# Two heads in one product: attention of an eight-head Fourier layer with the heads on two halves of the rows

## The chip, the core and the metric

The kernel runs on one core of a Trainium2 chip. The metric is the time of one execution in microseconds of the device; lower is better. A core has five engines that run side by side: TensorE (PE in the profile) multiplies matrices into the PSUM memory, VectorE (DVE) and ScalarE (ACT) work element by element and read PSUM, GpSimd (POOL) works element by element on SBUF, and SyncE (SP) issues the transfers. A product on TensorE has two operands: the stationary one, loaded into the array as weights, and the moving one, which streams past it. The contraction runs over the rows (partitions) of both, at most 128. A product that needs only some rows and columns of the array can be given a place in it, so that products at different places run side by side.

## What is computed

Two layers of the same kind, one behind the other, on an input `x` of 2 batches, 56 channels and 128 x 128 points. Cut to what matters:

```python
B, K, H, W = x.shape            # 2, 56, 128, 128
A = Kw.shape[2]                 # 8 heads
xn = inorm(x.reshape(B * K, 1, H, W), g1, b1)
k, q, v = (fno_layer(xn, w, b, sw, sb) for ... in (K, Q, V))     # each 8 heads
scores = jnp.einsum('baks,bals->bakl', qh, kh) * scale           # over the 128 x 128 points
attn = jax.nn.softmax(scores, axis=-1)                           # 56 x 56 for each head
out = jnp.einsum('bakl,bals->baks', attn, vh)
out = fno_layer(out.reshape(B * K, A, H, W), Pw, Pb, Psw, Psb)   # 8 heads to one
att = inorm(out + x, gan, ban)
an = inorm(att, g2, b2)
h = fno_layer(an, M0w, ..., norm=True, act=True)
h = fno_layer(h, M1w, ..., norm=True, act=False)
y = inorm(h, gmo, bmo) + att
```

`fno_layer` is a spectral convolution on 32 x 16 complex Fourier modes plus a 1 x 1 convolution. Everything is fp32.

## The kernel before

The work is done on the modes, not on the points, wherever it can be. For a batch `b`, the tile `xf` holds the modes of the 56 channels: 128 rows (64 for each half `e` of the modes) by 8 groups of 56 channels. Each layer runs through these stages, for batch 0 and batch 1, one stage of one batch woven with another stage of the other batch (`_woven` takes pieces of both generators in turn, by the costs that they yield; a planner then orders the instructions of each engine and inserts the waits):

- `turn`, `modes_chain`: mean and variance, the forward transform into `xf`.
- `gram`, `gram_chain`: a 56 x 56 product of the channels over all points (L511: 128 products of 128 rows by 64 columns, alternately on the lower and upper half of the columns).
- `scores`: for each of 8 mode groups and 8 heads a product of weights with the modes (L595), copied by ACT (L600), and then the scores (L576). They gather in one PSUM bank, heads 0 to 3 on rows 0 to 55 and heads 4 to 7 on rows 64 to 119. At its start POOL writes two masks that hold a scaled identity for each head: SG (L569) and MI (L570), each 56 rows by 8 x 56.
- `values`: for each pair `t` of mode groups (4 of them), halves `e` and members `c` a product with all 8 heads at once (L617), 64 rows by 64 columns with 512 moving columns; ACT copies 128 x 1024 to VT (L622). The modes' group is what distinguishes the two halves of VT's rows. At its end 8 transposes (L626) and a copy (L627).
- `softmax_chain`: DVE and ACT turn the scores into weights; 16 products with the identity (L648) transpose them, each head on both halves of the rows of PSUM, and ACT copies 128 x 448 to AT (L653).
- `mix_chain`: 8 products of the mask MI with AT (L661), one for each head, contracting 56 rows, and one product of two identities (L662), all summed into one bank; then BT (DVE, L665), L668, BTx (ACT, L670), L672, gb (DVE, L674) and 8 products (L678) into a bank that stays in use until `norms_chain`.
- `heads`: for each `t`, head `a`, half `e` and member `c` a product of VT and AT (L689), 56 rows by 64 columns with 56 moving columns, at one of four quadrants of the array; 128 products for each batch, summed over the heads. ACT copies the sum to D (L697).
- `norms_chain`, `gelu`, `h_chain`, `end`: the norms, the two further convolutions, and the result. `inverse` (L401, L406) and `gelu`'s synthesis (L751, L766) need pairs of PSUM banks too.

An fp32 product of the code is two instructions on PE, with two loads of weights. PSUM is given out from two pools: `bank()`, 2 tiles of one bank, and `pair()`, 3 tiles of two banks. Before the change, the transposed weights (`softmax_chain`) and the sums of `heads` each take a pair; the scores, the products of `mix_chain` and those of the norms take single banks.

The order around the change, in each layer (L946 to L961): `gram_chain` of batch 1 with `scores` of batch 0; `softmax_chain` with `values` of batch 0; `mix_chain` with `heads` of batch 0; `norms_chain` of batch 0 with `scores`, then `softmax_chain` with `values`, then `mix_chain` with `heads` of batch 1; `norms_chain` of batch 1 with `gelu` of batch 0. In `mix_chain` with `heads`, a quarter of the heads' products stands after L662's bank is read, a quarter after L672, and the rest behind L678.

Of the kernel before, what the change touches and what calls it, by code (L numbers as in the profile page):

```python
# [39 lines left out]
ALU = mybir.AluOpType  # L40
# [126 lines left out]
def fno_layers(ctx: ExitStack, tc: tile.TileContext, x, out, weights, small, const):  # L167
# [441 lines left out]
    def values(L, b, st):  # L609
        R, xf = room(b), st["xf"]  # L610
        xv = grid(xf[:, :448])
        for t in range(4):
            p = pair()
            for e in range(2):
                for c in range(2):
                    o = K * (2 * t + c)
                    T.matmul(  # L617
                        p[64 * c : 64 * c + 64, e, :], lhsT=xf[64 * e : 64 * e + 64, o : o + 64],
                        rhs=WTv[64 * e : 64 * e + 64, 2 * t + c].rearrange("p a m -> p (a m)"), start=True, stop=True,
                        tile_position=(64 * e, 64 * c), skip_group_check=True,  # L620
                    )
            S.copy(R["VT"][:, t], p.rearrange("p e m -> p (e m)"))  # L622
            yield 1.0
        p = pair()
        for t in range(8):
            T.transpose(p[:K, t // 4, N * (t % 4) : N * (t % 4) + N], xv[:, t, :], ident)  # L626
        S.copy(R["XT"][:K].rearrange("p t m -> p (t m)"), p[:K].rearrange("p j m -> p (j m)"))  # L627
        yield 0.8

    def softmax_chain(L, b, st):  # L630
        R, sc = room(b), st["sc"]
        SC = R["SC"][:, :, :K]
        rl, rk = st["rr"][:, :K], st["rr"][:, K : K + 1]
        V.tensor_tensor(SC, grid(sc[:, :224], 4), _bc(rl, 1, 4), ALU.mult)
        top, tot = little(f"top{b}", [N, 4]), little(f"tot{b}", [N, 4])
        V.tensor_reduce(top, SC, AX.X, ALU.max)
        V.tensor_tensor(SC, SC, _bc(top, 2, K), ALU.subtract)
        S.activation(SC, SC, AF.Exp, scale=rk)
# [14 lines left out]
        S.activation(R["AT"].rearrange("p (c m) -> p c m", c=2), p[:, :, :224], AF.Copy, scale=rk)  # L653
        yield 1.0

    def mix_chain(L, b, st):
        R, gc = room(b), st["gc"]
        AT, MI, XT = grid(R["AT"]), R["MI"], R["XT"]
        p = bank()
        for a in range(HEADS):  # L660
            T.matmul(p[:K, :K], lhsT=MI[:K, a, :], rhs=AT[:K, a, :], start=(a == 0), stop=False)  # L661
# [18 lines left out]

    def heads(L, b, st):
        R = room(b)
        AT, VT = grid(R["AT"]), R["VT"].rearrange("p t (e m) -> p t e m", e=2)
        p = pair()
        for t in range(4):
            for a in range(HEADS):
                for e in range(2):
                    for c in range(2):
                        T.matmul(  # L689
                            p[64 * e : 64 * e + 64, c, K * t : K * t + K],  # L690
                            lhsT=VT[64 * c : 64 * c + K, t, e, 64 * a : 64 * a + 64],
                            rhs=AT[64 * c : 64 * c + K, a, :], start=(a == 0), stop=(a == 7),
                            tile_position=(64 * c, 64 * e), skip_group_check=True,
                        )
# [330 lines left out]
```

## Time and profile before

| what | value |
|---|---|
| median of 3 runs (lowest to highest) | 573.26 us (572.86 to 574.89) |
| the profiled execution | 573.63 us |
| its span, first to last instruction | 571.6 us |
| mean granted clock of TensorE | 0.882 |

The profile lists, for each engine, the time in which it was busy, and for groups of instructions the line of the code, the operation, the tiles with their shapes (`56*64 56x56` is 56 rows by 64 columns of weights and 56 rows by 56 moving columns), the count, the busy time and the mean length of one. A chain of waits follows the execution back from its end: each piece is what the next had to wait for. The granted clock is the share of full speed that TensorE is allowed; it changes during the execution. Instructions of PE overlap in its pipeline, so that the mean length of one says less than how many start in a given time.

### The profile page before, as it was taken

The page shows a single profiled execution, that of the slowest core. Times are in us where ns is not written, and L with a number is a line of the kernel's source. Part 1 is how long each engine was busy: PE and PEld are TensorE (multiplying, and loading weights), DVE is VectorE, ACT ScalarE, POOL GpSimd, SP SyncE. Part 2 cuts the span into 40 slices and gives each one's busy share as a digit, 9 for nine tenths or more (in the row PEclk, how much of TensorE's full clock was granted, in tenths as well). Part 3 has the DMA queues.
Part 4 walks back from the last instruction along what each step waited for, and adds up shares of the span by engine and source line. Part 5 has one row for each costly group of instructions (what it writes and reads, how often), then busy time and mean ns, then how long its engine had stood idle before and what let it go on. Part 6 is the DMA issues. An engine that isn't in the chain of part 4 may idle for free.

```text
span 571.6 us, 15727 instructions
## 1 busy us (share of the span) xinstructions
PE 468.0 (82%) x7110; PEld 323.5 (57%) x7110; DVE 334.5 (59%) x577; ACT 191.1 (33%) x238; POOL 181.9 (32%) x190
## 2 busy tenths in 40 slices
PE   2547988989989999799596769987998999979390
PEld 1423957659676556466562367756957655645250
DVE  0576488811626765858459985830251866686751
ACT  2334140152428556123104214124352755612000
POOL 2440517800090000064456841810000000016466
PEclk9999699887999998977577959987799999899587
DMA  8993000050000000056145441030000000006587
GB/s 203 211 195 43 4 2 4 4 140 4 1 4 2 1 2 1 1 168 189 47 128 152 139 131 7 4 102 2 3 1 3 2 1 1 2 18 203 186 252 278
DMA packets 16307, 40.64 MB, mean 71 GB/s; under 512 B 2528, under 2 KB 3296, under 8 KB 16224
## 3 DMA queue, kind: packets, MB, share of 16 engines
q1 hardware_dynamic: 15520, 38.25, 24.9%
q10 hardware_dynamic: 720, 1.39, 1.0%
q8 instruction: 56, 0.92, 0.7%
q14 instruction: 11, 0.09, 0.1%
HBM read 24.69 MB, written 14.68 MB: 69 GB/s over the span
## 4 chain that ended last, share of the span: by engine, by line
PE 48%; DVE 25%; DMA 8%; ACT 7%; issue 5%; POOL 4%; SPq 1%; POOLq 1%; ACTq 0%; DVEq 0%
PE pair L766 6%; PE pair L751 5%; PE pair L595 4%; PE pair L801 4%; PE pair L689 4%; DVE X L550 4%; DVE stats L373 4%; PE bank L576 3%; PE bank L511 3%; PE bank L789 2%; DVE P L916 2%; DMA X<-store 2%; PE bank L483 2%; PE bank L386 2%; DMA sm<-small 2%
## 5 line engine op out<-in xcount | busy, mean ns | idle before, releaser
L821 DVE BATCH_NORM_STATS2 stats<-P 128x6 f32<-128x512 f32 x64 | 40.4, 677 | 20.2 <-ACT P L819 20.1
L916 DVE SCALAR_TENSOR_TENSOR P<-P,hs,pair 128x1024 f32<-128x1024 f32 x32 | 40.0, 1271 | 19.9 <-PE pair L766 19.8
L918 POOL TENSOR_TENSOR X<-P,xr 128x1024 f32<-128x1024 f32 x16 | 39.4, 2466 | 31.1 <-DVE P L916 20.0
L550 DVE TENSOR_TENSOR X<-X,gvr 120x1024 f32<-120x1024 f32 x32 | 48.9, 1558 | 0.0
L373 DVE BATCH_NORM_STATS2 stats<-P 128x6 f32<-128x448 f32 x64 | 35.7, 611 | 21.5 <-ACT P L371 11.9
L819 ACT ACTIVATE P<-pair 128x1024 f32<-128x1024 f32 x32 | 32.7, 1027 | 32.1 <-PE pair L766 31.5
L395 POOL MEMSET WT<- 128x256 f32 x4 | 1.3, 313 | 124.7 <-PE bank L789 90.3
L801 PEld LDWEIGHTS pair<-C,P 120*128 120x128 f32 x256 | 27.5, 146 | 21.4 <-issue 11.5
L511 PE MATMUL bank<-P 128*64 128x56 f32 (+1 forms) x1024 | 38.7, 243 | 0.0
L511 PEld LDWEIGHTS bank<-P 128*64 128x64 f32 (+1 forms) x1024 | 37.1, 158 | 2.2 <-issue 1.9
L766 PE MATMUL pair<-X,Be 57*64 57x512 f32 x256 | 38.2, 692 | 0.0
L751 PE MATMUL pair<-C,WT 32*128 32x128 f32 x512 | 29.2, 333 | 10.7 <-DVE P L916 5.2
L766 PE MATMUL pair<-X,Bs 57*64 57x512 f32 x256 | 37.6, 628 | 0.0
L595 PEld LDWEIGHTS pair<-xf,WU 64*64 64x64 f32 x1024 | 33.3, 138 | 5.0 <-issue 4.1
L595 PE MATMUL pair<-xf,WU 64*64 64x56 f32 x1024 | 36.1, 223 | 0.0
L801 PE MATMUL pair<-C,P 120*128 120x120 f32 x256 | 35.4, 282 | 0.7 <-ACT P L819 0.5
L751 PEld LDWEIGHTS pair<-C,WT 32*128 32x128 f32 x512 | 23.6, 225 | 21.6 <-DVE P L916 7.2
L363 PE MATMUL pair<-C,X 56*128 56x56 f32 x256 | 17.8, 297 | 18.6 <-DMA X<-x 12.8
L802 ACT COPY WT<-pair 128x896 f32<-128x896 f32 x32 | 28.8, 907 | 12.2 <-PE pair L801 11.9
L341 POOL TENSOR_TENSOR WT<-tc,C 128x1024 f32<-128x1024 f32 x8 | 26.5, 3344 | 20.0 <-ACT tc L335 11.9
L371 ACT COPY P<-pair 128x896 f32<-128x896 f32 x16 | 14.4, 903 | 46.5 <-PE pair L365 45.7
L365 PE MATMUL pair<-C,X 120*128 120x120 f32 x128 | 20.5, 314 | 10.8 <-POOL X L918 9.0
(249 smaller groups left out, 881.2 us busy)
## 6 DMA issues: line engine op xcount, KB each, us to landing
X<-x SPq DMA_DIRECT2D x16, 448.0 KB
xr<-x SPq DMA_DIRECT2D x32, 224.0 KB
store<-X SPq DMA_DIRECT2D x32, 224.0 KB
out<-P SPq DMA_DIRECT2D x32, 224.0 KB
xr<-store SPq DMA_DIRECT2D x16, 224.0 KB
X<-store SPq DMA_DIRECT2D x16, 224.0 KB
C<-const_all ACTq DMA_DIRECT2D x1, 621.0 KB
stage<-weights ACTq DMA_DIRECT2D x1, 544.0 KB
```

The costliest lines, as they stand in the source:

```text
L373: V.bn_stats(stats[:, 2 * g + s, :], dst[:, 448 * s : 448 * s + 448])
L511: T.matmul(p[u : u + m, :K], lhsT=P[b][:, K * i : K * i + m], rhs=plane[b][:, i, :], start=(i < 2), stop=(i == N - 1), tile_position=(0, u ...
L550: V.tensor_tensor(v, v, _bc(st["gvr"][:120], 1, 8), ALU.mult)
L595: T.matmul(p[64 * e : 64 * e + 64, k, K * a : K * a + K], lhsT=WUv[64 * e : 64 * e + 64, t + k, a, :], rhs=xv[64 * e : 64 * e + 64, t + k, ...
L751: T.matmul(both[j // 2][:, j % 2, N * e : N * e + N], lhsT=Z[32 * j : 32 * j + 32, o : o + N], rhs=C["gw"][32 * j : 32 * j + 32, :], start ...
L766: T.matmul(p[64 * c : 64 * c + 64, r, :], lhsT=Bs[q, :], rhs=X2[q, b, s : s + 4, :].rearrange("p e w -> p (e w)"), start=False, stop=True, ...
L801: T.transpose(p[:, r, N * e : N * e + 120], h3[:120, o : o + N], ident[:120, :120])
L802: S.copy(hT[v].rearrange("p r e c k -> p (r e) c k"), p.rearrange("p r (e c k) -> p (r e) c k", e=4, c=2)[:, :, :, :K],)
L819: S.activation(h3, both[v].rearrange("p r m -> p (r m)"), AF.Gelu)
L821: V.bn_stats(stats[:, 4 * A + 2 * v + r, :], h3[:, 512 * r : 512 * r + 512])
L916: V.scalar_tensor_tensor(h3, h3, st["hs"], both[v].rearrange("p r m -> p (r m)"), ALU.mult, ALU.add)
L918: G.tensor_tensor(dst, h3, back(n), ALU.add)
```

## The change

The upper half of the rows no longer holds another group of modes but other heads: rows 0 to 63 hold heads 0 to 3, rows 64 to 127 heads 4 to 7, as in the scores. A product of `mix_chain` or `heads` then contracts two heads at once, over 128 rows.

- `values`: L617's 512 columns (8 heads) become two products of 256 columns (4 heads for each half of the rows), 32 products instead of 16 for each batch; VT keeps its size.
- `softmax_chain`: 8 transposing products instead of 16, each head only on its own half; one bank instead of a pair; the copy to AT is 128 x 224.
- `mix_chain`: 4 products with MI over 128 rows instead of 8 over 56. The product of identities runs over 128 rows.
- `heads`: 64 products of 128 rows by 64 columns, alternately on the two column halves of the array, instead of 128 products of 56 rows on four quadrants; one bank instead of a pair; the copy to D keeps its size and has plain order.
- `scores`: the mask MI is written by two POOL instructions of 64 rows by 4 x 56 instead of one of 56 rows by 8 x 56.

```diff
-            "AT": R[:, 5120:5568], "SC": grid(R[:, 6912:7168], 4), "SG": grid(R[:, 7168:7616]),
-            "MI": grid(R[:, 7616:8064]), "UX": [R[:, 896 * j : 896 * j + 896] for j in range(2)],
+            "AT": R[:, 5120:5344], "SC": grid(R[:, 6912:7168], 4), "SG": grid(R[:, 7168:7616]),
+            "MI": grid(R[:, 7616:7840], 4), "UX": [R[:, 896 * j : 896 * j + 896] for j in range(2)],
...
     def scores(L, b, st):
...
-        G.tensor_tensor(MI[:K], _bc(ident[:K, :K], 1, HEADS), _bc(d["mix"][:K], 2, K), ALU.mult)
+        for c in range(2):
+            q = slice(64 * c, 64 * c + 64)
+            G.tensor_tensor(MI[q], _bc(C["fold"][q, :K], 1, 4), _bc(d["mix"][q, 4 * c : 4 * c + 4], 2, K), ALU.mult)
...
     def values(L, b, st):
...
-            for e in range(2):
-                for c in range(2):
-                    o = K * (2 * t + c)
-                    T.matmul(
-                        p[64 * c : 64 * c + 64, e, :], lhsT=xf[64 * e : 64 * e + 64, o : o + 64],
-                        rhs=WTv[64 * e : 64 * e + 64, 2 * t + c].rearrange("p a m -> p (a m)"), start=True, stop=True,
-                        tile_position=(64 * e, 64 * c), skip_group_check=True,
-                    )
+            for u in range(2):
+                for e in range(2):
+                    for c in range(2):
+                        o = K * (2 * t + u)
+                        T.matmul(
+                            p[64 * c : 64 * c + 64, e, 256 * u : 256 * u + 256], lhsT=xf[64 * e : 64 * e + 64, o : o + 64],
+                            rhs=WTv[64 * e : 64 * e + 64, 2 * t + u, 4 * c : 4 * c + 4].rearrange("p a m -> p (a m)"),
+                            start=True, stop=True, tile_position=(64 * e, 64 * c), skip_group_check=True,
+                        )
...
     def softmax_chain(L, b, st):
...
-        p = pair()
+        p = bank()
         for a in range(4):
             for c in range(2):
-                for r in range(2):
-                    T.matmul(
-                        p[64 * r : 64 * r + 64, c, K * a : K * a + K], lhsT=R["SC"][64 * c : 64 * c + K, a, :],
-                        rhs=ident[64 * c : 64 * c + K, 64 * c : 64 * c + K], start=True, stop=True,
-                        tile_position=(64 * c, 64 * r), skip_group_check=True,
-                    )
-        S.activation(R["AT"].rearrange("p (c m) -> p c m", c=2), p[:, :, :224], AF.Copy, scale=rk)
-        yield 1.0
+                q = slice(64 * c, 64 * c + K)
+                T.matmul(
+                    p[64 * c : 64 * c + 64, K * a : K * a + K], lhsT=R["SC"][q, a, :], rhs=ident[q, q], start=True, stop=True,
+                    tile_position=(64 * c, 64 * c), skip_group_check=True,
+                )
+        S.activation(R["AT"], p[:, :224], AF.Copy, scale=rk)
+        yield 0.8
 
     def mix_chain(L, b, st):
...
-        for a in range(HEADS):
-            T.matmul(p[:K, :K], lhsT=MI[:K, a, :], rhs=AT[:K, a, :], start=(a == 0), stop=False)
-        T.matmul(p[:K, :K], lhsT=ident[:K, :K], rhs=ident[:K, :K], start=False, stop=True)
+        for a in range(4):
+            T.matmul(p[:K, :K], lhsT=MI[:, a, :], rhs=AT[:, a, :], start=(a == 0), stop=False)
+        T.matmul(p[:K, :K], lhsT=ident[:, :K], rhs=ident[:, :K], start=False, stop=True)
...
     def heads(L, b, st):
...
-        p = pair()
-        for t in range(4):
-            for a in range(HEADS):
+        p = bank()
+        for t in range(8):
+            for a in range(4):
                 for e in range(2):
-                    for c in range(2):
-                        T.matmul(
-                            p[64 * e : 64 * e + 64, c, K * t : K * t + K],
-                            lhsT=VT[64 * c : 64 * c + K, t, e, 64 * a : 64 * a + 64],
-                            rhs=AT[64 * c : 64 * c + K, a, :], start=(a == 0), stop=(a == 7),
-                            tile_position=(64 * c, 64 * e), skip_group_check=True,
-                        )
-            yield 1.4
+                    T.matmul(
+                        p[64 * e : 64 * e + 64, K * t : K * t + K], lhsT=VT[:, t // 2, e, t % 2, a, :], rhs=AT[:, a, :],
+                        start=(a == 0), stop=(a == 3), tile_position=(0, 64 * e), skip_group_check=True,
+                    )
+            if t % 2:
+                yield 1.0
...
-        S.copy(D.rearrange("p (t c k) -> p c t k", c=2, k=K), p[:, :, :224].rearrange("p c (t k) -> p c t k", t=4))
+        S.copy(D, p[:, :448])
```

More of the change, by code (lines that the diff above doesn't have):

```diff
@@ L642, in softmax_chain @@
         yield 4.5
-        p = pair()
+        p = bank()
         for a in range(4):
             for c in range(2):
-                for r in range(2):
-                    T.matmul(
-                        p[64 * r : 64 * r + 64, c, K * a : K * a + K], lhsT=R["SC"][64 * c : 64 * c + K, a, :],
-                        rhs=ident[64 * c : 64 * c + K, 64 * c : 64 * c + K], start=True, stop=True,
-                        tile_position=(64 * c, 64 * r), skip_group_check=True,
-                    )
-        S.activation(R["AT"].rearrange("p (c m) -> p c m", c=2), p[:, :, :224], AF.Copy, scale=rk)
-        yield 1.0
+                q = slice(64 * c, 64 * c + K)
[5 more added lines that the diff above has]
+        yield 0.8
     def mix_chain(L, b, st):
         R, gc = room(b), st["gc"]
-        AT, MI, XT = grid(R["AT"]), R["MI"], R["XT"]
+        AT, MI, XT = grid(R["AT"], 4), R["MI"], R["XT"]
         p = bank()
-        for a in range(HEADS):
-            T.matmul(p[:K, :K], lhsT=MI[:K, a, :], rhs=AT[:K, a, :], start=(a == 0), stop=False)
-        T.matmul(p[:K, :K], lhsT=ident[:K, :K], rhs=ident[:K, :K], start=False, stop=True)
+        for a in range(4):
+            T.matmul(p[:K, :K], lhsT=MI[:, a, :], rhs=AT[:, a, :], start=(a == 0), stop=False)
+        T.matmul(p[:K, :K], lhsT=ident[:, :K], rhs=ident[:, :K], start=False, stop=True)
         BT = little(f"BT{b}", [K, 64])
@@ L682, in heads @@
         R = room(b)
-        AT, VT = grid(R["AT"]), R["VT"].rearrange("p t (e m) -> p t e m", e=2)
-        p = pair()
-        for t in range(4):
-            for a in range(HEADS):
+        AT, VT = grid(R["AT"], 4), R["VT"].rearrange("p t (e u a m) -> p t e u a m", e=2, u=2, a=4)
+        p = bank()
+        for t in range(8):
+            for a in range(4):
                 for e in range(2):
-                    for c in range(2):
-                        T.matmul(
-                            p[64 * e : 64 * e + 64, c, K * t : K * t + K],
-                            lhsT=VT[64 * c : 64 * c + K, t, e, 64 * a : 64 * a + 64],
-                            rhs=AT[64 * c : 64 * c + K, a, :], start=(a == 0), stop=(a == 7),
-                            tile_position=(64 * c, 64 * e), skip_group_check=True,
-                        )
-            yield 1.4
+                    T.matmul(
[4 more added lines that the diff above has]
+                yield 1.0
         D = st["D"] = sp.tile([N, 448], F32, name=f"D{b}")
-        S.copy(D.rearrange("p (t c k) -> p c t k", c=2, k=K), p[:, :, :224].rearrange("p c (t k) -> p c t k", t=4))
+        S.copy(D, p[:, :448])
     def norms_chain(L, b, st):
```

## The prediction

> **What bounds the kernel now.** I read the page first, then the groups by line, then the chain of waits in the two stretches where the changed functions run, then windows with the granted clock.
>
> ```profile
> span 571.6 us, 15727 instructions
> PE 468.0 (82%) x7110; PEld 323.5 (57%) x7110; DVE 334.5 (59%) x577; ACT 191.1 (33%) x238; POOL 181.9 (32%) x190
> PEclk9999699887999998977577959987799999899587
> ```
>
> PE is busy for 82% of the span, and PEclk falls below 9 in many slices: TensorE is the bound most of the time, but at a clock that changes. The change touches these groups, but for L511, which is there for comparison (each product of the code is two instructions; behind the first bar stand busy us and mean ns of one):
>
> ```profile
> L689 PE MATMUL pair<-P 56*64 56x56 f32 x1024 | 24.6, 264 | 0.0
> L617 PE MATMUL pair<-WT,xf 64*64 64x512 f32 x128 | 20.8, 605 | 2.3 <-DVE P L406 1.9 <-ACT P L622 0.4
> L661 PE MATMUL bank<-P 56*56 56x56 f32 x64 | 4.9, 236 | 5.0 <-ACT P L653 5.0
> L511 PE MATMUL bank<-P 128*64 128x56 f32 (+1 forms) x1024 | 38.7, 243 | 0.0
> L653 ACT ACTIVATE P<-pair,rr 128x448 f32<-128x448 f32 x4 | 2.5, 633 | 0.0
> L638 ACT ACTIVATE P<-P,rr 128x224 f32<-128x224 f32 x4 | 1.9, 482 | 3.4 <-DVE P L637 3.4
> ```
>
> Each runs four times: layers 0 and 1, batches 0 and 1. The chain of waits through layer 0 (start, length) shows what ends last:
>
> ```profile
> 112.49 1.00 PE pair L617 x2
> ...
> 114.40 1.00 PE pair L617 x2
> ...
> 117.76 1.01 ACT P L622
> ...
> 123.28 0.54 ACT P L653
> ...
> 123.86 1.74 PE bank L661 x16
> ...
> 130.18 3.59 PE bank L678 x16
> 133.76 3.40 PE pair L689 x128
> 137.16 1.87 PE pair L595 x64
> ...
> 161.53 1.03 PE bank L661 x16
> ...
> 167.04 2.02 PE pair L689 x128
> ```
>
> So the values' copies on ACT end last up to L653, and from L661 on PE alone does, through `mix_chain` and `heads`. Layer 1 repeats it:
>
> ```profile
> 381.49 1.00 PE pair L617 x2
> ...
> 391.91 1.06 PE bank L661 x16
> ...
> 401.14 3.61 PE pair L689 x128
> ...
> 429.91 1.03 PE bank L661 x16
> ...
> 435.42 2.02 PE pair L689 x128
> ```
>
> The same 128 instructions of L689 take 3.4 to 3.6 us for batch 0 and 2.02 for batch 1. The windows say why (length, PE busy, granted clock, DMA):
>
> ```profile
> 385.96:389.38 3.42, 2.11 (x19) 1.00 0.00 0
> 389.38:392.79 3.41, 1.84 (x54) 1.00 0.00 0
> 392.79:396.20 3.41, 3.41 (x100) 0.50 0.02 5
> ...
> 403.03:406.44 3.41, 3.41 (x102) 0.50 0.02 5
> 406.44:409.86 3.42, 3.42 (x123) 1.00 0.02 5
> ```
>
> After a window in which PE was busy for only 1.84 us the clock is 0.50 for four windows; 2.11 did not bring it down. Layer 0 does the same after 1.39 busy:
>
> ```profile
> 119.70:123.10 3.40, 1.39 (x39) 1.01 (x36) 0.95 (x3) 3.39 (x5) 0.00 (x0) 1.00 0.75 183
> ...
> 124.10:136.10 12.00, 12.00 (x257) 11.57 (x258) 0.43 (x3) 0.21 (x1) 0.41 (x2) 0.50 0.01 3
> ```
>
> The whole of batch 0's heads therefore runs at half clock, and batch 1's at full clock.
>
> **The change part by part.** Heads: 256 instructions per run become 128, each with 128 rows of weights instead of 56 and still 64 columns by 56. Four quadrants of the array become two column halves. The trace has the new form already: the gram product of L511 (128*64, 128x56, alternating column halves). The rows of both, in order of time:
>
> ```profile
> 360.61 2.08 PE L511 MATMUL bank<-P 128*64 128x56 f32 x64
> ...
> 166.97 2.09 PE L689 MATMUL pair<-P 56*64 56x56 f32 x128
> ...
> 401.07 3.68 PE L689 MATMUL pair<-P 56*64 56x56 f32 x128
> 338.00:341.00 3.00, 3.00 (x62) 3.00 (x62) 2.81 (x4) 0.15 (x1) 1.48 (x2) 0.50 0.47 129
> ```
>
> At full clock, less one instruction's own length (0.24 and 0.26 from the groups), L511 starts one every 1.84/63 = 29.2 ns and L689 one every 1.83/127 = 14.4: two for one. At half clock L689 takes (3.68 - 0.26)/127 = 27. L511 has 62 instructions that touch a window of 3.0 us; each lasts some 0.3 (an estimate: 0.243 is its mean over both clocks), so one starts every 3.3/62 = 53 ns: again two for one. Half as many at twice the price: 128 x 29.2 = 3.74 against 256 x 14.4 = 3.69 us. I take **0** for the heads, bounds -0.3 to +0.3 each (the chain's 2.02/128 = 15.8 gives -0.3).
>
> [...]
>
> Mix: L661 goes from 16 instructions to 8 on one place of the array, where nothing overlaps: half of 1.74, 1.06, 1.03 and 1.03, **-2.4**. The identity product of L662 stays at two instructions. Bounds: 0 (if 128 rows cost double, which L511 speaks against) to -2.4.
>
> Softmax: 32 transposing instructions on four quadrants become 16 on the two diagonal ones, by the same two-for-one no change; they end before the ACT copy L627 anyway. L653 halves to 128x224; the nearest row is L638 of that shape, 482 against 633 ns, four times on the chain: **-0.6**.
>
> Values: 32 instructions of 512 columns become 64 of 256, the same columns. At four quadrants the extra starts cost some ns each; bounds 0 to +0.2 each, mostly under the ACT copies; I take **+0.1** in all. But three times a lone product of L617 stands in the chain between scores, 1.00 us for two instructions in one quadrant; half as wide it takes 0.5. At most -0.5 each, at least 0 if two halves are put there in turn on one quadrant; what is put off costs a little later; I take **-0.6** in all.
>
> PSUM: the heads' sums and the transposed weights leave the three pairs for the two single banks. While the heads hold one bank, L668, L672 and L678 share the other, and L672 must wait for the copy of L668's result:
>
> ```profile
> 128.15 0.21 ACT L670 COPY BTx<-bank 128x64 f32<-128x64 f32 x1 [4.33 <-PE bank L668]
> ```
>
> If L672 stands right behind L668 in PE's queue, all heads products wait behind it 0.21 us and two handovers, some 0.3; if a quarter of the heads goes ahead, nothing. Bounds 0 to +1.2 in all; I take **+0.3**. L678 needs L674's read as well, with a quarter of the heads between: 0. Pairs set free could let `scores` of batch 1 start in the PE gap before L661; no row shows it now, so it belongs to a rival.
>
> POOL: the mask product becomes two of 64x224:
>
> ```profile
> 125.73 0.31 POOL L395 MEMSET P<- 128x256 f32 x1 [13.08 <-PE bank L661]
> ```
>
> POOL is idle 13 us there, so a second instruction is hidden; uncovered it would cost under 1 us. The D copy L697 keeps its 128x448.
>
> Sum before the clock: -2.4 - 0.6 - 0.6 + 0.1 + 0.3 = -3.2. Of this some 2.1 falls to batch 0 (half of 1.74 and 1.06, two L653, the lone products, less 0.2), before or in the half-clock stretch. That stretch's end is a window's end (406.44 above), not the end of the heads: what is saved lets `scores` (L595) start earlier at half clock, so only half is kept: +1.05. Net **-2.2**. The profiled execution took 573.63 (span 571.6 and 2.0 around it), 0.37 over the median 573.26 of the runs. 573.63 - 2.2 - 0.37 = 571.1 us.
>
> [...]
>
> **The rivals.** *The stretch stays warm.* Layer 1 goes cold on 1.84 us of PE work where 2.11 was enough. L653 ends 0.15 earlier, the values earlier still, and freed pairs may fill the gap with L595. If that tips it, the four windows run at full clock: 13.65/2 = 6.8 less, with the 0.5 given back in that layer: about 565 us; in both layers about 558.5. Against: layer 0 has only 1.39, and everything also shifts against the windows.
>
> *Nothing arrives.* L672 stalls (+0.9 more), the lone L617 stay, 128 rows cost something in the mix: about 573.0.
>
> *Slower: the clock later on.* From the heads on everything shifts by one to three us against windows that stand still. Between 239 and 345 us PE has long gaps:
>
> ```profile
> 235.78:239.19 3.41, 3.02 (x52) 1.00 0.02 5
> 239.19:242.61 3.42, 1.38 (x16) 1.00 0.00 0
> 242.61:246.02 3.41, 3.21 (x36) 0.50 0.00 0
> ```
>
> Each further window that falls below about 2 us of work costs the next one half its 3.41, 1.7 us. Three more make 571.1 + 5.1 = 576.2. It decides from the third on; one or two only eat the gain. For it: such windows are there now. Against: a shift removes one as easily as it makes one.
>
> *The count is the bound.* If heads were paid by the instruction, batch 1 saves 2.0 each and batch 0 3.4, half of which returns: 571.1 - 4.0 - 3.4 = 563.7. L511 speaks against it. [...]
>
> **How the numbers follow.** Forecast 0.47 (own range 568.5 to 573.6), warm stretch 0.22 (both layers 0.05 of it), nothing arrives 0.11, clock later on 0.14, count 0.05, loads 0.01. A measurement of this kernel can tell about 0.5% from no change, 2.87 us: 570.4 and 576.1. Of the forecast 0.18 lies below 570.4 and 0.02 above 576.1. Faster 0.18 + 0.22 + 0.05 = 0.45; same 0.27 + 0.11 = 0.38; slower 0.02 + 0.14 + 0.01 = 0.17. The range runs from 563.5, below one warm layer, to 575.5; both layers warm, the third rival and the loads are left out, under 0.2.
>
> **What would show it.** Right: the new heads at 29 ns a start at full and 53 at half clock, so as long as now; L661's eight at half their time; L653 near 480 ns; the clock at 0.50 through batch 0's heads in both layers. Wrong: a clock of 1.00 there (time falls by 6 us a layer), heads starts near 15 or above 60 ns, PE idle before L672, or L595 ahead of L661.

## The result, and the profile after

The changed kernel takes 557.28 us (median of 4 runs, 556.93 to 558.51) against 574.08 of the kernel before beside it (572.86 to 574.93): a ratio of 0.9713, 95% interval 0.9686 to 0.9740. That is faster by 16.8 us, and 6 us below the predicted range. Its profiled execution took 556.93 us, that of before 573.63. Here and below, ratios leave out executions more than 1.5% above the fastest of their kernel; medians and ranges hold all.

The page of the changed kernel answers to the lines shown of before:

```profile
span 555.1 us, 14768 instructions
PE 457.0 (82%) x6630; PEld 316.3 (57%) x6630; DVE 337.0 (61%) x577; ACT 190.2 (34%) x238; POOL 184.3 (33%) x194
PEclk9999689899998999988667959989999999988586
```

TensorE (PE) is still busy for 82%, but its clock falls less often: the slices in which batch 0's heads run (the ninth and tenth, the 28th and 29th) had 8, 7, 7 and 7 and have 9 now. The groups by line (the lines moved by two: L617 is L620, L653 is L655, L661 is L663, L678 is L680, L689 is L690):

```profile
L690 PE MATMUL bank<-P 128*64 128x56 f32 x512 | 20.4, 235 | 0.0
L620 PE MATMUL pair<-WT,xf 64*64 64x256 f32 x256 | 19.8, 384 | 2.4 <-DVE P L406 1.9 <-ACT P L625 0.5
L663 PE MATMUL bank<-P 128*56 128x56 f32 x32 | 2.5, 220 | 1.2 <-ACT P L655 1.2
L655 ACT ACTIVATE P<-bank,rr 128x224 f32<-128x224 f32 x4 | 1.8, 447 | 0.0
```

The mix is down from 4.9 to 2.5 us, the copy of the weights from 633 to 447 ns. The heads went from 24.6 to 20.4 us. The chain of waits through layer 0 says why:

```profile
113.97 0.57 PE pair L620 x2
...
115.45 0.57 PE pair L620 x2
...
116.58 1.01 ACT P L625
...
119.38 2.73 ACT P L625 x3
...
123.00 0.35 ACT P L655
...
123.40 0.62 PE bank L663 x8
...
125.05 0.36 PE bank L670 x2
125.42 0.48 PE bank L690 x10
125.90 0.23 PE bank L674 x2
...
126.97 1.92 PE bank L680 x16
128.89 2.03 PE bank L690 x64
```

The last 64 instructions of the heads take 2.03 us, as before's 128 took at full clock (2.02), and L680 takes 1.92 where before's L678 took 3.59. The windows with the granted clock (length, PE, weight load, DVE, ACT and POOL busy, then clock, DMA):

```profile
123.40:131.00 7.60, 7.60 (x164) 7.17 (x165) 0.43 (x3) 0.27 (x2) 0.41 (x2) 1.00 0.02 6
384.13:387.55 3.42, 3.42 (x55) 3.18 (x52) 0.21 (x1) 0.10 (x1) 0.00 (x0) 1.00 0.03 5
387.55:390.96 3.41, 3.41 (x66) 3.31 (x66) 0.00 (x0) 0.00 (x0) 0.00 (x0) 0.50 0.00 0
390.96:394.37 3.41, 3.33 (x108) 3.24 (x110) 1.87 (x3) 2.30 (x4) 0.68 (x1) 1.00 0.03 5
```

Batch 0's heads of layer 0 run at 1.00 from end to end, and those of layer 1 have one window at half clock in place of four. That window follows one in which TensorE was busy all the time, 1.99 of the 3.42 us with L680, whose products all use one place of the array. The windows ahead of the heads, in layers 0 and 1, answer to the prediction's 1.39 and 1.84 us busy:

```profile
121.31:124.72 3.41, 2.94 (x86) 2.80 (x85) 0.21 (x1) 2.03 (x3) 0.31 (x1) 1.00 0.45 124
380.72:384.13 3.41, 3.06 (x81) 2.80 (x78) 0.21 (x1) 1.30 (x3) 0.31 (x1) 1.00 0.00 0
```

Where the 16.7 us between the two profiled executions lie can be read from rows on ScalarE: batch 1's `rr` (L543), and for each batch the weights' copy (L653, now L655) and the heads' copy (L697). In layer 0 up to batch 0's heads, before and after:

```profile
111.81 0.32 ACT L543 ACTIVATE rr<-bank,eps 128x57 f32<-128x57 f32 x1
...
117.76 1.01 ACT L622 COPY P<-pair 128x1024 f32<-128x1024 f32 x1 [0.79 <-PE pair L617]
...
123.18 0.64 ACT L653 ACTIVATE P<-pair,rr 128x448 f32<-128x448 f32 x1
...
137.24 0.53 ACT L697 COPY D<-pair 128x448 f32<-128x448 f32 x1 [8.88 <-PE pair L689]
```

```profile
113.29 0.32 ACT L543 ACTIVATE rr<-bank,eps 128x57 f32<-128x57 f32 x1
...
122.89 0.45 ACT L655 ACTIVATE P<-bank,rr 128x224 f32<-128x224 f32 x1
130.94 0.53 ACT L697 COPY D<-bank 128x448 f32<-128x448 f32 x1 [5.28 <-PE bank L690]
```

| Stage (us, from start to start) | before L0, L1 | after L0, L1 | gain |
|---|---|---|---|
| `rr` of batch 1 to the weights of batch 0 | 11.37, 14.83 | 9.60, 12.93 | 3.7 |
| weights to heads' copy, batch 0 | 14.06, 13.59 | 8.05, 9.53 | 10.1 |
| from there to the weights of batch 1 | 23.61, 24.42 | 23.21, 23.20 | 1.6 |
| weights to heads' copy, batch 1 (full clock) | 8.28, 8.28 | 8.04, 8.04 | 0.5 |

At full clock mix and heads gain 0.24 us a time. So of the 10.1 us of batch 0 some 9.6 (10.1 - 2 x 0.24) are clock. Of the 1.6 us of the third row 0.8 are clock too: in layer 1 the half-clock stretch of before runs from the heads' copy (404.81) 1.6 us on, to 406.44, and the row is 0.8 us longer there than in layer 0. That makes some 10.4 us of clock, and the work of the rows is 3.7 + 0.8 + 1.0 = 5.5. The other 0.9 lies outside. (In layer 1 the first row holds part of a half-clock window in both kernels, at a mean clock of 0.91 and 0.92.)

### The profile page after: what moved, and what is told of

Read it like the earlier page. It is cut to its first block, busy times and chain, and to the rows that moved or that the text cites. A ratio compares the mean times of both kernels' runs of the same rounds, so it can differ in the third digit from the quotient of the medians.

```text
span 555.1 us, 14768 instructions
## 1 busy us (share of the span) xinstructions
PE 457.0 (82%) x6630; PEld 316.3 (57%) x6630; DVE 337.0 (61%) x577; ACT 190.2 (34%) x238; POOL 184.3 (33%) x194
## 3 DMA queue, kind: packets, MB, share of 16 engines
q10 hardware_dynamic: 720, 1.39, 1.0%
## 4 chain that ended last, share of the span: by engine, by line
PE 43%; DVE 26%; DMA 8%; ACT 7%; POOL 7%; issue 5%; SPq 2%; POOLq 0%; ACTq 0%; DVEq 0%
PE pair L766 5%; DVE X L550 4%; PE pair L801 4%; PE pair L751 4%; PE pair L597 4%; DVE stats L373 4%; PE bank L511 3%; PE bank L578 3%; DMA C<-const_all 3%; DMA X<-store 3%; POOL P L918 3%; PE bank L690 3%; PE bank L789 2%; PE bank L483 2%; DMA xr<-store 2%
## 5 line engine op out<-in xcount | busy, mean ns | idle before, releaser
L373 DVE BATCH_NORM_STATS2 stats<-P 128x6 f32<-128x448 f32 x64 | 35.7, 610 | 20.1 <-ACT P L368 10.1
L766 PE MATMUL pair<-X,Be 57*64 57x512 f32 x256 | 41.1, 742 | 0.0
L751 PE MATMUL pair<-C,WT 32*128 32x128 f32 x512 | 26.7, 319 | 11.3 <-DVE P L916 5.5
L597 PE MATMUL pair<-xf,WU 64*64 64x56 f32 x1024 | 35.9, 220 | 0.0
L597 PEld LDWEIGHTS pair<-xf,WU 64*64 64x64 f32 x1024 | 32.8, 134 | 5.0 <-issue 3.9
L751 PEld LDWEIGHTS pair<-C,WT 32*128 32x128 f32 x512 | 21.6, 214 | 23.6 <-issue 9.1
L371 ACT COPY P<-pair 128x896 f32<-128x896 f32 x16 | 14.4, 902 | 46.7 <-PE pair L365 46.7
```

The source lines that it names most:

```text
L373: V.bn_stats(stats[:, 2 * g + s, :], dst[:, 448 * s : 448 * s + 448])
L597: T.matmul(p[64 * e : 64 * e + 64, k, K * a : K * a + K], lhsT=WUv[64 * e : 64 * e + 64, t + k, a, :], rhs=xv[64 * e : 64 * e + 64, t + k, ...
L751: T.matmul(both[j // 2][:, j % 2, N * e : N * e + N], lhsT=Z[32 * j : 32 * j + 32, o : o + N], rhs=C["gw"][32 * j : 32 * j + 32, :], start ...
L766: T.matmul(p[64 * c : 64 * c + 64, r, :], lhsT=Bs[q, :], rhs=X2[q, b, s : s + 4, :].rearrange("p e w -> p (e w)"), start=False, stop=True, ...
```

## The experiments

After the result there were two theories. **A**: pairs set free let the scores of batch 1 fill the gap ahead of the mix, and that holds the clock. **B**: the new products do it themselves. Later theories grew out of the misses. Time is the median of the run's executions; the ratio is to the kernel before on the same chip (572.7 to 574.0 us). "Stage" is weights to heads' copy of batch 0 in layers 0 and 1, with the granted clock, in the profiled execution; there is one of these for each kernel, so these columns are one draw each.

| Run | us | ratio, 95% | stage L0, L1 | clock L0, L1 |
|---|---|---|---|---|
| e1 pairs again | 555.95 | 0.9685 (0.9617 to 0.9753) | 9.35, 7.81 | 0.81, 1.00 |
| e2 before + transposes | 565.71 | 0.9839 (0.9729 to 0.9949) | 14.23, 8.29 | 0.51, 1.00 |
| e3 before, scores early | 567.01 | 0.9878 (0.9832 to 0.9924) | 8.73, 8.73 | 1.00, 1.00 |
| e4 e1 + transposes | 556.53 | 0.9721 (0.9631 to 0.9810) | 7.81, 7.81 | 1.00, 1.00 |
| e5 after | 556.42 | 0.9707 (0.9679 to 0.9735) | 8.05, 9.48 | 1.00, 0.81 |
| e6 before, values split | 568.82 | 0.9892 (0.9843 to 0.9940) | 13.17, 12.45 | 0.56, 0.61 |
| e7 after, mix twice | 558.82 | 0.9772 (0.9724 to 0.9820) | 8.46, 9.94 | 1.00, 0.82 |
| e8 after, old heads | 562.13 | 0.9798 (0.9762 to 0.9834) | 12.42, 7.85 | 0.57, 1.00 |
| e9 e8 with 64 rows | 559.24 | 0.9738 (0.9705 to 0.9771) | 7.84, 7.85 | 1.00, 1.00 |
| e10 after, values in turns | 557.42 | 0.9709 (0.9685 to 0.9733) | 8.05, 8.05 | 1.00, 1.00 |
| e11 e6 with 64 rows | 566.07 | 0.9849 (0.9813 to 0.9885) | 8.29, 8.30 | 1.00, 1.00 |
| e12 input on two halves | 555.82 | 0.9676 (0.9642 to 0.9709) | 7.93, 7.94 | 1.00, 1.00 |
| e13 before + 128-row product | 563.05 | 0.9833 (0.9791 to 0.9876) | 9.72, 8.54 | 0.82, 1.00 |
| e14 before + 32-row product | 572.13 | 0.9980 (0.9945 to 1.0015) | 14.13, 13.71 | 0.51, 0.53 |
| e15 e12, mix on halves | 554.41 | 0.9676 (0.9633 to 0.9718) | 7.27, 7.28 | 1.00, 1.00 |

**The order of the work (e1, e5, e4, e3, e2).** e1 puts the sums in `softmax_chain` and in `heads` back into pairs, and with them PE's order of before:

```diff
-        p = bank()
+        p = pair()[:, 0, :]
...
```

> The changed kernel, but the transposed weights and the sums of heads take a pair of banks again, so that the planner's order on PE is that of before (no scores of batch 1 ahead of L663). Theory A (the freed pairs let PE work in the gap before the mix, and that keeps the clock at 1.00): the clock falls to 0.50 through the heads of batch 0 in both layers again, and the time is 567 to 571 us. Theory B (the fewer and wider products themselves): 557 to 559 us, as the changed kernel.

> The changed kernel as it is, beside the next three on one chip. The version that differs from it only in the buffers for the sums of the transposed weights and of the heads (pairs instead of single banks) took 555.95 us. If the buffers and the order of work that follows from them are worth nothing: 555.5 to 557.5 us here as well. If they are worth what I first thought: some 10 us below that other version, 546.

Measured 555.95 (554.32 to 556.37) and 556.42 us (556.11 to 558.84): the buffers and the order are worth nothing that shows. In e1 no L597 runs ahead of the mix, and the clock still holds but for one window in layer 0: theory A falls for the changed kernel. e2 and e4 add 16 needless transposes behind the real ones, to before and to e1 (first diff); e3 puts the first piece of the scores of batch 1 ahead of the mix of batch 0 in before (second).

```diff
+        warm = bank()
+        for _ in range(2):
+            for a in range(4):
+                for c in range(2):
+                    q = slice(64 * c, 64 * c + K)
+                    T.matmul(
+                        warm[64 * c : 64 * c + 64, K * a : K * a + K], lhsT=R["SC"][q, a, :], rhs=ident[q, q], start=True,
...
```

```diff
+        early = scores(L, 1, s1)
+        next(early)
...
-            norms_chain(L, 0, s0), _with(scores(L, 1, s1), scale_x(1, s1)),
+            norms_chain(L, 0, s0), _with(early, scaled),
```

> The kernel before, with 16 needless transposing products (32 instructions, about 0.95 us) behind L648, in the gap in which PE waits for ACT; nobody reads them. Theory A: PE is busy for over 2.1 us of the window before the mix, the clock stays at 1.00 through the heads of batch 0, and the time falls from 574 to 561 to 564 us. Theory B: 574 us or up to 2 us more.

> The first of these kernels (changed products, pairs taken again) with the needless products of the second in the gap. Theory A: clock at 1.00 again in batch 0's heads, 556 to 560 us. Theory B: no different from the first of these kernels, or slower by up to 2 us.

> The kernel before, with its own products; only the first piece of the scores of batch 1 (32 products, 64 instructions, 2.0 us) is put ahead of the mix by hand. Theory A: the gap is filled with useful work and the clock stays at 1.00; 559 to 563 us. Theory B: 573 to 574 us.

e2 (562.77 to 576.30) and e3 (563.99 to 575.82) missed their numbers, since the clock came back only in places: e2's in layer 1, e3's in both layers' batch 0, while batch 1 of layer 1 lost it (its stage took 12.55 us there instead of 8.28). e4 is e1 with the clock at 1.00 in both layers, and the two intervals overlap. Both filled gaps show that the clock of before can be held from outside; neither says by what.

**Parts of the change (e6, e7, e8).** e6 is before with values products of 256 columns in place of 512; e7 the changed kernel with eight mix products of half the weight; e8 the changed kernel with heads in the old form, which leaves out the addition of the lower and the upper rows' sums.

```diff
+            for u in range(2):
+                for e in range(2):
+                    for c in range(2):
...
+                            p[64 * c : 64 * c + 64, e, 256 * u : 256 * u + 256], lhsT=xf[64 * e : 64 * e + 64, o : o + 64],
+                            rhs=WTv[64 * e : 64 * e + 64, 2 * t + c, 4 * u : 4 * u + 4].rearrange("p a m -> p (a m)"),
```

```diff
-        ts(col("mix", 8), vp, par["g1"], None, ALU.mult)
+        ts(col("mix", 8), vp, par["g1"], 0.5, ALU.mult, ALU.mult)
...
-        for a in range(4):
-            T.matmul(p[:K, :K], lhsT=MI[:, a, :], rhs=AT[:, a, :], start=(a == 0), stop=False)
+        for n in range(8):
+            T.matmul(p[:K, :K], lhsT=MI[:, n // 2, :], rhs=AT[:, n // 2, :], start=(n == 0), stop=False)
```

```diff
...
+                    for c in range(2):
+                        q = slice(64 * c, 64 * c + K)
+                        T.matmul(
+                            p[64 * e : 64 * e + 64, c, K * t : K * t + K], lhsT=VT[q, t, e, a // 4, a % 4, :],
+                            rhs=AT[q, a % 4, :], start=(a == 0), stop=(a == 7), tile_position=(64 * c, 64 * e),
...
```

> The kernel before, with one thing taken from the change: each values product of 512 columns is issued as two of 256 (the same columns, the same results). Theory 1, the lone half-width product ahead of the mix is what both shortens the stage before it and leaves TensorE less idle there: the stage from the gram mask's row to the transposed weights is 1.8 us shorter in each layer, the clock stays at 1.00 through batch 0's heads in at least one layer, 560 to 566 us. Theory 2, the clock stays up because the mix or the heads themselves have changed: only the shorter stage, 568 to 571 us, and 0.50 through batch 0's heads in both layers.

> The changed kernel, with the mix matrix halved and each of its four products issued twice, so that the mix has eight products again (the results stay the same). If the eight sparse products of the mix are what let the clock fall in the kernel before: 0.50 through batch 0's heads again, about 6 us more a layer, 562 to 570 us. If they are not: 4 products of some 64 ns per instruction, twice a layer and at full clock, 0.5 us for each mix, 2 us in all at most: 557 to 559 us, with the clock at 1.00.

> The changed kernel, with the heads issued in the old form: 256 instructions per run on four quadrants with 56 rows of weights, in place of 128 on two column halves with 128 rows. The sums of the lower and the upper rows stay apart in two banks and are not added, so the output lacks that sum. If the new form of the heads keeps the clock up: 0.50 through the heads of batch 0 in at least one layer, 562 to 569 us. If the form is indifferent, as 29 ns a start against 14.4 say: 555 to 558 us, and the heads of batch 1 as long as in the changed kernel within 0.3 us.

e6 took 568.82 us (562.27 to 572.10), what theory 2 gave: the stage from `rr` to the weights is 9.60 and 13.28 us, as short as in the changed kernel in layer 0, but the clock falls as before in the profiled execution. e6's windows in layer 1 (the one ahead of the stretch at half clock, then the next):

```profile
388.37:391.78 3.41, 2.34 (x84) 2.23 (x84) 0.21 (x1) 1.02 (x2) 0.31 (x1) 1.00 0.02 5
391.78:395.20 3.42, 3.42 (x74) 3.30 (x73) 0.21 (x1) 0.21 (x1) 0.00 (x0) 0.50 0.00 0
```

2.34 us busy let the clock fall here, where 2.11 did not in before: busy time does not order these windows. e7 put 0.4 us on each mix (8.46 against 8.05 in layer 0) and left the clock (1.00 and 0.82, e5 1.00 and 0.81): its sparse products are not the cause. e8 took 562.13 us, in the range given for the case that the new form of the heads keeps the clock up: at full clock its stage is 7.85 us, 0.04 from the new form's 7.81 in e1 (which keeps the heads in a pair too), but layer 0 lost the clock. Windows of layer 0 of e8, then of e1, each time the one in which the weights are copied and the next:

```profile
120.98:124.39 3.41, 2.01 (x69) 1.76 (x70) 0.21 (x1) 2.08 (x3) 0.31 (x1) 1.00 0.63 166
124.39:127.81 3.42, 3.42 (x105) 3.15 (x96) 0.22 (x2) 0.21 (x1) 0.00 (x0) 0.50 0.02 5
```

```profile
120.15:123.56 3.41, 2.01 (x53) 1.82 (x48) 0.21 (x1) 1.58 (x3) 0.31 (x1) 1.00 0.58 141
123.56:126.97 3.41, 3.41 (x54) 3.16 (x53) 0.22 (x2) 0.21 (x1) 0.00 (x0) 1.00 0.02 5
```

Both were busy for 2.01 us, e8 with more instructions, and e8 alone went to half clock in the next window (e1 lost it for one window behind the second one shown). The two kernels differ in their heads: e8's products have 56 rows, e1's 128; the number and the place of the products differ too.

e5, e6 and e8 ran beside one another on one chip, so that their ratios make a ladder. Before to e6 (values split) is 1.1% or some 6 us, e6 to e8 (weights, mix and their layout) 0.9% or 5 us, e8 to the changed kernel (heads) another 0.9%, 5 us. No one part brings the gain, and taken in this order the heads bring a third of it though they take the same time at full clock.

**Rows (e9, e11, e13, e14).** e9 and e11 give the old heads eight more rows, in which the moving operand is zero, in e8 and e6 (e9's edit, against e8):

```diff
-                        q = slice(64 * c, 64 * c + K)
+                        q = slice(64 * c, 64 * c + 64)
...
```

> The version with the heads in the old form (562.13 us, TensorE at half clock through batch 0's heads of layer 0), where each of its 256 products takes 64 rows instead of 56; the eight more rows are zeros, so the sums are the same, and again the two halves' sums aren't added. Theory rows: what holds the clock is how many rows a stretch of products streams (rows times columns; 56x56 per 14.4 ns in the old form is 218 a ns, 128x56 per 29.2 ns in the new one 245, 64x56 per 14.4 ns would be 249). Then 555 to 558 us with at most one half-clock window in batch 0's heads of each layer. Theory form (256 short products on four quadrants against 128 on two column halves): no change, 560 to 564 us, with several half-clock windows in one layer.

> The kernel before with its values products split (568.82 us, half clock through batch 0's heads in both layers), and 64 rows instead of 56 in each of its 256 heads products (zeros, the same sums). Theory rows: layer 1, whose window ahead of the cold stretch held 66 such products, stays at 1.00, layer 0, with 35 of them, may not: 560 to 565 us. Theory form: 567 to 570 us, half clock in both layers.

The zeros cost no time (stages of 7.84 and 7.85 us against 7.85 in e8, at full clock). By the medians the kernels are faster by 2.9 and 2.8 us, each against its parent on another chip; the intervals of the ratios touch for e9 and overlap widely for e11, so the first gain is at the edge of the noise and the second within it. The profiled executions keep full clock through batch 0's heads. e9's window with the weights' copy, and the next:

```profile
121.65:125.06 3.41, 2.01 (x86) 1.82 (x86) 0.21 (x1) 1.80 (x3) 0.31 (x1) 1.00 0.63 151
125.06:128.47 3.41, 3.41 (x102) 3.22 (x93) 0.23 (x2) 0.21 (x1) 0.00 (x0) 1.00 0.02 5
```

Again 2.01 us, and the clock stays. But e9's window ends 0.28 us later behind the start of the weights' copy than e8's does, and so holds more products as well as more rows. And by their medians both stand between the two theories (e9 555.81 to 561.82; e11 560.67 to 568.17, with the profiled execution the fastest). So one more pair was made, in which only the rows differ: before, with one needless product in the gap ahead of the mix.

```diff
+        warm = bank()
+        T.matmul(warm, lhsT=ident[:128, :], rhs=Ct[:128, :512], start=True, stop=True)
```

e14 has 32 in place of both 128.

> The kernel before with one needless product put behind the transposes of the weights, into TensorE's gap ahead of the mix: 128 rows by 512 columns, about 1.0 us in two instructions, its result unused. Theory rows (what holds the clock is rows times columns streamed in a window): the windows ahead of batch 0's mix go from about 215 and 225 thousand to 346 and 356, above the 278 thousand that parts warm from cold best in the profiles so far; 1.00 through batch 0's heads in both layers, 560 to 564 us. Theory busy time (how long TensorE has something under way): the same, for 1.4 and 1.8 us busy become 2.4 and 2.8. If the gap ahead of the mix isn't the cause: 573 to 575 us.

> The same needless product at the same place with the same 512 columns, but 32 rows in place of 128: as long, a quarter of the rows. Theory rows: 248 and 258 thousand, still cold, half clock through batch 0's heads in both layers, 571 to 575 us. Theory busy time: as with 128 rows, 560 to 564 us.

The product's group in e13 and in e14 (one instruction 644 and 650 ns: as long), and the window that holds it in layer 1, with the next:

```profile
L654 PE MATMUL bank<-C 128*128 128x512 f32 x8 | 4.5, 644 | 0.0
```

```profile
L654 PE MATMUL bank<-C 32*128 32x512 f32 x8 | 4.6, 650 | 0.0
```

```profile
384.86:388.27 3.41, 2.90 (x51) 1.80 (x50) 0.00 (x0) 2.75 (x4) 0.00 (x0) 1.00 0.00 0
388.27:391.68 3.41, 3.41 (x145) 3.17 (x143) 0.42 (x2) 0.21 (x1) 0.31 (x1) 1.00 0.02 5
```

```profile
390.60:394.01 3.41, 2.89 (x53) 1.79 (x52) 0.00 (x0) 2.63 (x4) 0.00 (x0) 1.00 0.00 0
394.01:397.42 3.41, 3.41 (x94) 3.19 (x96) 0.26 (x2) 0.21 (x1) 0.31 (x1) 0.50 0.02 5
```

With 2.90 and 2.89 us busy the clock stays at 128 rows and falls at 32. The time is 563.05 us (561.11 to 566.01) against 572.13 (569.41 to 575.31). A product of no use makes before 10.7 us faster by the medians (9.6 by the ratio). Theory busy time falls; between these two the rows decide. In layer 0 e13 still lost one window further on (0.82 in the table), where theory rows gave 1.00; e14 is cold in both layers, as given.

How the clock counts is not settled by that. Rows times streamed columns, summed over the products that start in a window, give 331 thousand for e13's window and 226 for e14's, 250 for e8's, and 314 for e9's and e1's. The changed kernel's windows ahead of the heads have 437 in both layers, and its full window in layer 1 that lost the clock has 271. But in layer 1 windows of 229 (e8), 240 (e11) and 243 thousand (e1) stayed warm, and 264 (e6) fell; in layer 0 e1's full window above fell with 300 where the changed kernel's stayed with 299. Over the 1997 full-clock windows of all 17 profiles, 256 of them followed by half clock, the best bound on this count, 279 thousand, misjudges 90, the best on busy time 114: closer, not a law.

**The lone products (e10).**

```diff
-            for u in range(2):
-                for e in range(2):
-                    for c in range(2):
+            for e in range(2):
+                for c in range(2):
+                    for u in range(2):
...
```

> The changed kernel with the values products of one pair in another order: the two of 256 columns that share a quadrant stand behind each other, so that a lone one between pieces of the scores holds the chain as long as one of 512 columns did. Theory, the stage before the mix is shorter because a lone product is half as wide: the stage from the gram mask's row to the transposed weights is up to 1.8 us longer again in each layer, 558 to 560 us if the clock stays. If the order in the pair is indifferent: 556 to 557 us and 9.6 us for that stage in layer 0.

e10's chain in layer 0 has one lone piece as long as before's and one as short as the changed kernel's:

```profile
114.05 1.00 PE pair L620 x4
115.05 0.91 PE bank L578 x8
115.96 0.57 PE pair L620 x2
```

The stage from `rr` is 10.04 us there, 0.44 over the changed kernel's: one piece's 0.43. In layer 1 the stage is 11.93 us, 1.05 shorter than e5's and not longer; e10 has a clock of 1.00 there, e5 0.92, so that layer can't be read for the pieces. The 557.42 us (556.05 to 559.09) can't be told from e5's. So by layer 0 the width of the lone pieces is worth some 0.4 us each; what else shortens the stage is ScalarE's 0.79 us wait for L617 (the row of before above), which is gone.

**Carried on (e12, e15).** L680 takes 1.92 us for 16 instructions at one place of the array. e12 puts the transposed input (even and odd channels) and the mix matrix on both halves of the rows too; e15 makes that mix on two column halves in turn.

```diff
...
-            T.matmul(pb[:, K * t : K * t + K], lhsT=XT[:K, t, :], rhs=BT[:, :K], start=True, stop=True)
+            h, q = t % 2, slice(64 * (t % 2), 64 * (t % 2) + K)
+            T.matmul(
+                pb[:, h, K * (t // 2) : K * (t // 2) + K], lhsT=XT[q, t // 2, :], rhs=BT[q, :K], start=True, stop=True,
+                tile_position=(64 * h, 0), skip_group_check=True,
+            )
...
```

> The changed kernel, carried on: the transposed input that the mix is applied to lies on two halves of the rows as well (even and odd channels), and the mix matrix is made on both halves, so that the eight products of it that take 1.9 us at full clock (120 ns an instruction, nothing overlapping) run on two row halves in turn, and the copy of that input on ScalarE, 1.01 us on the chain, is half as wide. If two row halves overlap as they do in the old heads: 16 instructions in about 1.0 us, 0.9 less four times, the copy 0.45 less four times, 551 to 553 us. If the load of 128 columns of weights is what sets 120 ns wherever the rows lie: only the copy, 554 to 556 us.

> The version with the transposed input on two halves of the rows (555.82 us), its mix issued on two column halves in turn (20 instructions) in place of one product of 128 columns of weights (10 instructions in 1.10 + 0.39 us): at the 29 ns a start of two column halves 20 instructions take 0.8 us, 0.6 less for each of four mixes. 553 to 555 us, and the stage from the weights' copy to the heads' copy 7.3 us in place of 7.93 at full clock. If small products on column halves cost what one of L663 does (64 ns), no change: 555 to 557 us.

PE in e12 (mix, then the products that were L680) and in e15:

```profile
120.40 1.10 PE L670 MATMUL bank<-P 128*128 128x56 f32 x8 [0.97 <-ACT P L662]
...
124.64 1.10 PE L688 MATMUL pair<-BT,P 56*128 56x56 f32 x16
```

```profile
122.32 0.68 PE L668 MATMUL bank<-P 128*64 128x56 f32 x16 [0.97 <-ACT P L659]
...
125.90 1.10 PE L689 MATMUL pair<-BT,P 56*128 56x56 f32 x16
```

The sixteen instructions take 1.10 us instead of 1.99 (`L680`, first start to last end); e12 gives half of that back to a mix with 128 columns of weights (1.10 against 0.62), and its 555.82 us (553.01 to 561.44) missed the 551 to 553 that went with the overlap; e15 doesn't (0.68). e15's stage is 7.27 us as expected, and with 554.41 us (553.08 to 556.29) it has the lowest median, below both kernels. The intervals of e15's and e5's ratios overlap, so only its lead over before is certain.

## Why the prediction was wrong

- **The step that failed**: "That stretch's end is a window's end (406.44 above), not the end of the heads", with the clock at 0.50 through batch 0's heads. It took the half-clock stretch as given and gave +1.05 back to it. In the changed kernel the stretch is gone but for one window in layer 1. The profiled executions put the clock at some 10.4 us; e13, which only adds a needless product to before, gains 10.7 by the medians.
- The rival **the stretch stays warm** (558.5 us for both layers, chance 0.05) gave the time. Its reasons were half right. That freed pairs let L597 fill the gap is true of the trace, but without it the time is the same (e1). Earlier values alone didn't do it in e6's profiled execution. Shown is that rows streamed ahead of the heads can hold the clock (e13 against e14), and that the new form of the heads is worth 0.9% with the same time at full clock (e8 against e5). That it is so because they stream 128 rows where the old had 56 fits e9 and e11, but their gains are at the edge of the noise or within it; what in the new weights and mix brings the other 0.9% is not split further.
- Two things misled. The prediction took the windows of before as they stood (1.39 and 1.84 us busy) and held layer 0's 1.39 too far off to tip; in the changed kernel those ahead of the heads have 2.94 and 3.06, more than the 2.11 that it had itself seen to be enough. And the measure is poor: 2.01 us held the clock in e1 and lost it in e8, 2.34 lost it in e6. With 2.90 us busy e13 held it, with 2.89 e14 lost it. So the "about 2 us of work" below which the prediction let a window cost the next one half was its estimate from 2.11 and 1.84, and these windows don't bear it out.
- **Heads, 0 us**: right. 64 instructions in 2.03 us against 128 in 2.02, one every 28.5 ns ((2.03 - 0.235)/63) where 29 were taken, and e8's stage of 7.85 us in the old form against e1's 7.81 in the new. The rival "the count is the bound" is out. The chance of 0.01 for the loads rested on nothing that a run shows; by these times the new form is no slower than the old.
- **Softmax, -0.6**: right, 447 ns for L655 where 482 were taken, so 0.7.
- **Mix, -2.4**: right in L663 (4.9 to 2.5 us), though part of it is clock. "Nothing overlaps" at one place of the array holds of the starts, as the records show them: L661's instructions last 212 ns and start 52 ns apart, L680's 272 and 112, where L689 on four quadrants starts one every 14.4. And each adds to the time: with eight more e7's L663 takes 0.41 us longer (1.03 for 16, 0.62 for 8). At full clock the stage gained 0.24, less than 0.41 for L663 and 0.19 for L655. With the sums in a pair it is 7.81 against 8.04 to 8.05 (e1, e4 and after): in the single bank ten heads instructions stand between L670 and L674, and from L670 up to L680 the chain takes 1.90 us (the lines above) against 1.66 in e1. **The bank wait, +0.3 in all**, was too small: no stall, but 0.24 us each, some 1.0 in all.
- **Lone products and values, -0.5 together**: mis-sized. The stage from `rr` gained 3.7 us over both layers (1.77 and 1.90). e6, which has only the split, shows the same 9.60 us in layer 0. There two lone pieces of 0.57 for 1.00 are 0.9 of the 1.8; the rest is ScalarE, which no longer waits for L617 between its copies (0.79 us). The prediction had priced PE's pieces and not the copy queue behind them.
- **Clock later on**: chance 0.14, not seen. Outside the rows of the table the two profiles differ by 0.9 us. The windows stand still within an execution only: all changes of the clock lie 3.41 us or a multiple of it apart in each of the two profiles, but the grids of before (406.44) and after (390.96) are shifted by 1.8 us.
- The 1.6 us between batch 0's heads and batch 1's weights was not foreseen. Half is the end of before's half-clock stretch in layer 1. The other half, 0.4 a layer, goes with the buffers: the stage is 23.2 us with single banks (after, e5) and 23.8 with pairs (e1, e4), at full clock. That about makes up for the 0.24 us of each mix, and so the buffers show no effect on the time.

## What to carry to other kernels

Where a clock falls in a gap, look at what the products in that window stream, not only at how long the engine was busy: here a product of 128 rows in the gap (644 ns an instruction) held the clock in layer 1, while one of 32 rows that took as long (650) did not. Before pricing a change in small products, ask at which clock the stage will run, and give each answer its own run. Small products that shared one place of the array (L680, 1.99 us for 16 instructions) gained by being put on two row halves (1.10 in e12 and e15).

## What the hardware showed that was not expected

- A window that is busy throughout can still lose the clock: the 3.42 us full window with L680 (384.13 above) was followed by 0.50. By rows times columns it has 271 thousand.
- Eight rows of zeros in each heads product cost nothing in time (stages of 7.84 and 7.85 us against 7.85), and with them the profiled executions kept the clock where those of the parents had lost it. By the medians the two kernels are 2.8 to 2.9 us faster, one at the edge of the noise, one within it.
- 32 and 128 rows of weights took about the same time: 650 and 644 ns an instruction of 512 columns.
- Before's time varies with the clock it is granted: beside e13, 578.65 us at a mean clock of 0.872 and 570.92 at 0.897. The changed kernel scatters less (556.1 to 558.8 us in e5, where before ran from 569.4 to 574.8 and once took 581.1). A profile is one draw of this.
